# The reciprocal root in the collecting: a bit guess and Newton's steps on VectorE in place of ScalarE's Sqrt and a reciprocal

## The chip, the cores and the metric

The kernel runs on one core of one Trainium2 chip. Its engines work from queues of their own: TensorE (PE, with its weight loads as PEld), VectorE (DVE), ScalarE (ACT), GpSimd (POOL) and SyncE (SP, used here to issue DMAs). The metric is the device time of one execution in microseconds (us); the time of a kernel is the median of its runs.

## The reference

The input x has two sequences of 4096 tokens with 512 values each. What is computed, in float32 throughout:

```python
# attention: a linear layer W that learns while it reads, one step of descent per token
K, V, Q = x @ theta_K.T, x @ theta_V.T, x @ theta_Q.T
for each token t:                                  # per sequence, W and b start from W0, b0
    g = 2/512 * (W @ K[t] + b - V[t])
    W, b = W - 0.01 * outer(g, K[t]), b - 0.01 * g
    y[t] = W @ Q[t] + b
x = layernorm(x + y)                               # (x - mean) / sqrt(var + 1e-5), over 512 values
# feed-forward: one shared expert, and the best 2 of 8 routed experts for each token
shared = silu(x @ sW1 + sb1) @ sW2 + sb2
score  = sqrt(softplus(x @ routing_W.T + expert_bias))
routed = sum over the 2 experts e of the highest score:
             score[e] * (silu(x @ rW1[e] + rb1[e]) @ rW2[e] + rb2[e])
out = layernorm(x + shared + routed)
```

The change is in the last of these lines: the factor 1 / sqrt(var + 1e-5) of the second layernorm, for all tokens but those of the last chunk.

## The kernel before

**Chunks and steps.** The 4096 tokens of a sequence are cut into 32 chunks of 128, and both sequences go together, so a chunk c is two blocks of 128x512 (s = 0, 1). Within a chunk the recurrence is turned into matrix products with a small triangular inverse; from chunk to chunk the matrices W go on. `step(c)` (from L420) does this for chunk c, with the first layernorm at its end (`layernorm`, L278). Beside it run `prep(c+1)` (projections of the next chunk), `invert(c)` (VectorE's row operations on the inverse, L373), and `shared(c-1)` (shared expert and `router` of the chunk before). A helper, `interleave`, weaves these generators in proportion to amounts given by hand; each `yield` is a place where it may go over to another.

**Routed experts.** Chunks 0 to 22 form the first group and 23 to 30 the second (`GROUPS`). The router writes down which tokens go to which expert. When a group is complete, `plan` makes lists of tiles of 128 tokens with one expert each, and `routed` works through the tiles: POOL gathers tokens (L812) and weights (L818) by indirect DMA; TensorE turns the tokens (L827) and makes the first product (L836); ScalarE applies Silu (`he`, L840); TensorE makes the second product (`pye`, L847); VectorE evicts it with a bias (`o`, L850), and SP's queue stores it (L852). A weight buffer is fetched anew only after the L850 that read it. Chunk 31 is left out of the groups: `dense(31)` computes all eight experts for it and weighs them (Silu L705, products L702 and L713, sum L716), with its own layernorm.

**Collecting.** `collect(gr)` brings a group's results back, chunk by chunk. For chunk j+1 POOL fetches `acc`, which is x plus the shared expert (L882), and four gathered tiles `z` (L888; two sequences, two experts). For chunk j VectorE adds the four `z` to `acc`, each with its weight (L933). Then the mean and the variance are formed, in one of two ways. With `squares` set, the last sums also give the row totals, VectorE scales them to minus the mean (L939), and ScalarE takes the squares with their totals (L941). Otherwise VectorE uses its statistics instructions (L946, L947). The end of a chunk is the generator `finish` (from L895): variance plus epsilon (L898 or L900), ScalarE's Sqrt in place (L901), `yield`, VectorE's reciprocal (L903), with `squares` the product of mean and factor (L905), the scaling of `acc` (L908 on ScalarE, or L911 on VectorE), and the output's DMA on ScalarE's queue (L913).

**Where `finish` stands.** It is not run at once: `done` holds it, and the next chunk's loop calls it twice, ahead of its sums number 2 and 3 (`finish_at` is (2, 3)), or number 0 and 1 in the stage without `squares`. So the part up to the `yield` stands in VectorE's order ahead of one L933, and the rest ahead of the next. For the last chunk of a group both parts follow at once.

**Stages.** The first group is collected in three places: 14 chunks in steps 28 to 31 (4, 4, 4 and 2, with `squares`), and 9 beside the second group's routed tiles (without `squares`). The second group's 8 chunks are collected at the end beside `dense(31)` (with `squares`).

**Order.** For TensorE and VectorE the order of instructions is the order in which the program is written (`manual_schedule`), so an instruction that waits holds all behind it on its engine. The orders of ScalarE, POOL and SP are laid by a scheduler when the program is built. ScalarE's functions come in tables; the compiler puts an `ACT_TABLE_LOAD` ahead of a function whose table isn't the one loaded. Sqrt is used by both layernorms (L286), the router (L547) and `finish` (L901); Exp (L517) and Ln (L522) by the router; Silu at L638, L705 and L840.

Of the kernel before, what the change touches and what calls it, by code (L numbers as in the profile page):

```python
# [41 lines left out]
F32 = mybir.dt.float32  # L42
BF16 = mybir.dt.bfloat16
I32 = mybir.dt.int32
AF = mybir.ActivationFunctionType
ALU = mybir.AluOpType
# [60 lines left out]
def postln_block(ctx: ExitStack, tc: tile.TileContext, x, xT, thK, thV, thQ, w0, b0, masks, blk,  # L107
                 unit, order, rw, eb, w1s, b1s, w2s, b2s, b2e, wcat, out):
    nc = tc.nc
# [24 lines left out]
    sm = ctx.enter_context(tc.tile_pool(name="sm", bufs=2))  # L134
# [138 lines left out]
    for g, n in enumerate(GROUPS):  # L273
        groups.append(Group(g, sum(GROUPS[:g]), n))
        for i in range(n):
            of_step[groups[g].c0 + i] = groups[g]

    def layernorm(t, tag, c, s, scalar=False):  # L278

        st = sm.tile([P, 6], F32, tag=tag + "st", name=f"{tag}st_{c}_{s}")  # L280
        nc.vector.bn_stats(st, t[:, s, :])
        mv = sm.tile([P, 2], F32, tag=tag + "mv", name=f"{tag}mv_{c}_{s}", bufs=3)
        nc.vector.bn_aggr(mv, st)
        rstd = sm.tile([P, 1], F32, tag=tag + "rs", name=f"{tag}rs_{c}_{s}", bufs=3)
        nc.vector.tensor_scalar(rstd, mv[:, 1:2], EPS, None, ALU.add)
        nc.scalar.activation(rstd, rstd, AF.Sqrt)  # L286
        yield
        nc.vector.reciprocal(rstd, rstd)
        if scalar:
            shift = sm.tile([P, 1], F32, tag=tag + "sh", name=f"{tag}sh_{c}_{s}")  # L290
            nc.vector.tensor_scalar(shift, mv[:, 0:1], rstd, -1.0, ALU.mult, ALU.mult)
            nc.scalar.activation(t[:, s, :], t[:, s, :], AF.Identity, bias=shift, scale=rstd)
        else:
            nc.vector.tensor_scalar(t[:, s, :], t[:, s, :], mv[:, 0:1], rstd,
                                    ALU.subtract, ALU.mult)
        yield
# [578 lines left out]
    def collect(gr):  # L875

        got = {}

        def fetch(j):
            c = gr.c0 + j  # L880
            acc = cp.tile([P, B, D], F32, tag="acc", name=f"acc_{c}", bufs=4)
            nc.gpsimd.dma_start(out=acc,  # L882
                                in_=gr.base[j * T:(j + 1) * T].rearrange("(s p) d -> p s d", p=P))
            z = []
            for s in range(B):
                for k in range(K):
                    t = cp.tile([P, D], F32, tag=f"z{s}{k}", name=f"z_{c}_{s}_{k}")
                    nc.gpsimd.indirect_dma_start(  # L888
                        out=t, out_offset=None, in_=gr.ex,
                        in_offset=bass.IndirectOffsetOnAxis(ap=gr.sidx[:, j, s, k:k + 1], axis=0),  # L890
                        bounds_check=gr.tiles * P - 1, oob_is_err=False)
                    z.append(t)
            got[j] = acc, z

        def finish(c, acc, mean, var, on_scalar):  # L895

            if on_scalar:
                nc.vector.tensor_scalar(var, var, 1.0 / D, EPS, ALU.mult, ALU.add)  # L898
            else:
                nc.vector.tensor_scalar(var, var, EPS, None, ALU.add)  # L900
            nc.scalar.activation(var, var, AF.Sqrt)  # L901
            yield
            nc.vector.reciprocal(var, var)  # L903
            if on_scalar:
                nc.vector.tensor_tensor(mean, mean, var, ALU.mult)  # L905
            for s in range(B):
                if on_scalar:
                    nc.scalar.activation(acc[:, s, :], acc[:, s, :], AF.Identity,  # L908
                                         bias=mean[:, s:s + 1], scale=var[:, s:s + 1])
                else:  # L910
                    nc.vector.tensor_scalar(acc[:, s, :], acc[:, s, :], mean[:, s:s + 1],  # L911
                                            var[:, s:s + 1], ALU.subtract, ALU.mult)
            nc.scalar.dma_start(out=out[:, c * P:(c + 1) * P, :].rearrange("s p d -> p s d"),  # L913
                                in_=acc)
            yield

        fetch(0)
        yield 2.0
        done = iter(())
        for j in range(gr.n):  # L920
            c = gr.c0 + j
            if j + 1 < gr.n:
                fetch(j + 1)
            acc, z = got.pop(j)
            on_scalar = squares[0]
            mv = sm.tile([P, 2, B], F32, tag="fmv", name=f"fmv_{c}")
            mean, var = mv[:, 0], mv[:, 1]

            for i in range(B * K):
                s, k = i // K, i % K  # L930
                if i in finish_at[0]:
                    next(done, None)
                nc.vector.scalar_tensor_tensor(  # L933
                    acc[:, s, :], z[i], gr.cw[:, j, s, k:k + 1], acc[:, s, :], ALU.mult, ALU.add,
                    accum_out=mean[:, s:s + 1] if on_scalar and k == K - 1 else None)
                yield 0.9
            if on_scalar:

                nc.vector.tensor_scalar(mean, mean, -1.0 / D, None, ALU.mult)  # L939
                for s in range(B):  # L940
                    nc.scalar.activation(z[s * K], acc[:, s, :], AF.Square,  # L941
                                         bias=mean[:, s:s + 1], accum_out=var[:, s:s + 1])
            else:
                for s in range(B):
                    st = sm.tile([P, 6], F32, tag="fst", name=f"fst_{c}_{s}")
                    nc.vector.bn_stats(st, acc[:, s, :])  # L946
                    nc.vector.bn_aggr(mv[:, :, s], st)  # L947
            for _ in done:
                pass
            done = finish(c, acc, mean, var, on_scalar)  # L950
            yield 0.4
        for _ in done:
            pass
# [110 lines left out]
```

## Time and profile before

| | |
|---|---|
| median of 3 runs | 2687.22 us (2684.12 to 2687.95) |
| the profiled execution | 2680.63 us |
| its span, first to last instruction | 2678.8 us |
| mean granted clock of TensorE | 0.982 |
| busy: PE / PEld | 2549.3 / 1648.3 us |
| busy: DVE / ACT / POOL | 1375.0 / 743.4 / 984.5 us |
| instructions: DVE / ACT | 4024 / 1480 |
| finishes in the trace | 31, at 2155 to 2673 us |

Busy time in us, stage by stage, for the part of the span in which the collecting runs:

| stage | from : to (us) | PE | DVE | ACT | POOL |
|---|---|---|---|---|---|
| step 28 | 2143 : 2210 | 61.9 | 46.2 | 22.2 | 27.7 |
| step 29 | 2210 : 2277 | 62.8 | 44.1 | 23.2 | 28.9 |
| step 30 | 2277 : 2344 | 56.7 | 49.2 | 30.2 | 28.1 |
| step 31 | 2344 : 2400 | 38.2 | 23.6 | 15.7 | 26.7 |
| routed tiles | 2400 : 2609 | 181.4 | 79.3 | 82.3 | 118.7 |
| last stage | 2609 : 2679 | 50.8 | 40.4 | 47.0 | 35.2 |

The busy time of an engine is read against the length of the stage: TensorE fills 62 of 67 us in step 28, and in the last stage no engine is full on its own. What holds the work there is seen from the waits and from the chain, which is followed back from the last instruction, at each step to what released it. "Idle before, <-" in a row names what ended the idle time ahead of an instruction; "issue" is time for which the trace shows no wait. Times in the trace's rows count from the start of the span.

### The profile page before, as it was taken

What the parts mean: (1) busy time and instruction counts of PE and PEld (TensorE: products, weight loads), DVE (VectorE), ACT (ScalarE), POOL (GpSimd) and SP (SyncE); (2) the same over time, 40 slices, a digit from 0 to 9 for tenths busy, and PEclk for the clock granted to TensorE, in tenths of its full rate; (3) what the DMA queues carried; (4) which work ended last, traced back from release to release, by engine and by line L of the source; (5) the groups of instructions that cost most, each with busy time, mean ns of one, the idle gap of its engine ahead of it and who ended that gap; (6) DMA issues with size and microseconds to landing.
All of it is one profiled execution on the core that took longest, in us unless ns stands there. A gap on an engine that the chain in (4) does not pass through costs nothing.

```text
span 2678.8 us, 30957 instructions
## 1 busy us (share of the span) xinstructions
PE 2549.3 (95%) x10269; PEld 1648.3 (62%) x10269; DVE 1375.0 (51%) x4024; ACT 743.4 (28%) x1480; POOL 984.5 (37%) x819
## 2 busy tenths in 40 slices
PE   8999999999999999999998989999999999879887
PEld 6656666665666666566665767666676655445564
DVE  2566656656666566666565223232232466744336
ACT  1222222222222222222221313323233133434236
POOL 0232322233332223233234344343443444456554
PEclk9999999999999999999999999999999999989898
DMA  5122222222222222222223333442433446586676
GB/s 182 48 78 73 57 65 68 57 58 78 73 57 61 72 57 58 71 79 58 59 64 134 107 95 109 110 158 82 114 106 104 135 142 176 162 257 228 216 244 231
DMA packets 257711, 293.47 MB, mean 110 GB/s; under 512 B 158332, under 2 KB 171868, under 8 KB 253968
## 3 DMA queue, kind: packets, MB, share of 16 engines
q1 hardware_dynamic: 199536, 163.62, 20.6%
q0 software_dynamic: 49584, 111.61, 14.6%
q10 hardware_dynamic: 8432, 16.25, 1.8%
q8 instruction: 82, 1.34, 0.2%
q14 instruction: 77, 0.63, 0.1%
HBM read 345.43 MB, written 100.69 MB: 167 GB/s over the span
## 4 chain that ended last, share of the span: by engine, by line
PE 82%; DMA 5%; issue 4%; DVE 3%; ACT 3%; POOL 2%; SPq 0%; POOLq 0%; DVEq 0%; ACTq 0%
PE pkq L330 16%; PE pr L431 8%; PE pr L436 8%; PE pye L847 8%; PE po L447 7%; PE pw L491 7%; PE phe L836 7%; PE ph L619 4%; PE pa L343 4%; PE py L659 4%; PE pe L473 2%; PE po L485 2%; PE pg L827 2%; PE pz L412 1%; DMA wb<-wcat_in,widx 1%
## 5 line engine op out<-in xcount | busy, mean ns | idle before, releaser
L373 DVE SCALAR_TENSOR_TENSOR X<-L,X 128x31 f32<-128x31 f32 (+22 forms) x1472 | 418.2, 333 | 26.4 <-DMA L<-dL 9.5
L836 PEld LDWEIGHTS phe<-gT,wb 128*128 128x128 f32 x2208 | 275.2, 197 | 80.9 <-issue 76.1
L586 POOL DMA_INDIRECT gt<-code,ri x124 | 128.1, 1033 | 494.4 <-DVE ri L583 465.2
L850 DVE TENSOR_TENSOR o<-pye,wb 128x512 f32<-128x512 f32 x138 | 95.4, 692 | 412.8 <-PE pye L847 409.4
L836 PE MATMUL phe<-gT,wb 128*128 128x128 f32 x2208 | 279.0, 281 | 23.5 <-DMA wb<-wcat_in,widx 22.1
L847 PE MATMUL pye<-wb,he 128*128 128x512 f32 x552 | 271.8, 615 | 16.1 <-ACT he L840 15.0
L481 POOL PARTITION_ALL_REDUCE ar<-R x28 | 172.3, 6155 | 237.4 <-issue 180.9
L491 PE MATMUL pw<-R,K 128*128 128x512 f32 x496 | 239.4, 605 | 13.5 <-DVE x L486 12.6
L330 PE MATMUL pkq<-xT,thK 128*128 128x256 f32 x1024 | 242.9, 381 | 7.4 <-DMA thK<-thK_in 7.4
L447 PE MATMUL po<-W,kq 128*128 128x512 f32 x512 | 246.5, 604 | 0.0
L330 PE MATMUL pkq<-xT,thQ 128*128 128x256 f32 x1024 | 243.8, 382 | 1.0 <-DVE Z L414 1.0
L330 PEld LDWEIGHTS pkq<-xT,thK 128*128 128x128 f32 x1024 | 195.1, 191 | 80.4 <-issue 59.5
L818 POOL DMA_INDIRECT wb<-wcat_in,widx x138 | 147.0, 1065 | 262.1 <-DVE o L850 133.5
L431 PE MATMUL pr<-thV,xT 128*128 128x512 f32 x512 | 240.5, 593 | 0.0
L436 PE MATMUL pr<-W,kq 128*128 128x512 f32 x512 | 240.2, 592 | 0.0
L330 PEld LDWEIGHTS pkq<-xT,thQ 128*128 128x128 f32 x1024 | 189.7, 191 | 46.6 <-issue 24.9
L840 ACT ACTIVATE he<-phe,wb 128x128 f32<-128x128 f32 x276 | 87.1, 364 | 435.8 <-PE phe L836 434.1
L492 DVE TENSOR_TENSOR W<-pw,W 128x512 f32<-128x512 f32 x248 | 168.5, 689 | 73.0 <-PE pw L491 70.4
L337 ACT COPY kq<-pkq 128x256 f32<-128x256 f32 x256 | 82.9, 375 | 420.5 <-PE pkq L330 420.2
L812 POOL DMA_INDIRECT g<-gy,gidx x138 | 138.8, 1006 | 134.0 <-PE pg L827 105.9
L491 PEld LDWEIGHTS pw<-R,K 128*128 128x128 f32 x496 | 91.3, 191 | 137.1 <-issue 95.6
L847 PEld LDWEIGHTS pye<-wb,he 128*128 128x128 f32 x552 | 99.5, 192 | 120.4 <-issue 81.8
(209 smaller groups left out, 3429.8 us busy)
## 6 DMA issues: line engine op xcount, KB each, us to landing
ge<-o SPq DMA_DIRECT2D x138, 256.0 KB, 2.0
xT<-xT_in SPq DMA_DIRECT2D x32, 512.0 KB, 4.3
x<-x_in SPq DMA_DIRECT2D x32, 512.0 KB, 4.3
L<-dL SPq DMA_DIRECT2D x128, 128.0 KB, 2.8
gy<-x SPq DMA_DIRECT2D x31, 512.0 KB, 3.0
gb<-x SPq DMA_DIRECT2D x31, 512.0 KB, 3.4
acc<-gb POOLq DMA_DIRECT2D x31, 512.0 KB, 5.3
y_out<-acc ACTq DMA_DIRECT2D x31, 512.0 KB, 5.1
```

Source lines behind the costliest of these rows:

```text
L330: nc.tensor.matmul(ps[:, i].rearrange("p s t -> p (s t)"), th[:, dc, (ec + i) * P:(ec + i + 1) * P], xt[:, dc].rearrange("p s t -> p (s t) ...
L373: nc.vector.scalar_tensor_tensor(X[:, h, j + 1:], L[:, j + 1:, j], X[:, h, j:j + 1], X[:, h, j + 1:], ALU.mult, ALU.add)
L431: nc.tensor.matmul(ps, xt[:, dc, s, :], nthV_sb[:, dc, :], start=(dc == 0), stop=False)
L436: nc.tensor.matmul(ps, KQ[:, ec, s, 0, :], W[s][:, ec, :], start=False, stop=(ec == DC - 1))
L447: nc.tensor.matmul(ps, KQ[:, ec, s, 1, :], W[s][:, ec, :], start=(ec == 0), stop=False)
L481: nc.gpsimd.partition_all_reduce(ar, R, P, bass_isa.ReduceOp.add)
L491: nc.tensor.matmul(ps, K[s][:, ec, :], F[s], start=True, stop=True)
L492: nc.vector.tensor_tensor(W[s][:, ec, :], ps, W[s][:, ec, :], ALU.add)
L812: nc.gpsimd.indirect_dma_start(out=g_t[k], out_offset=None, in_=gr.y, in_offset=bass.IndirectOffsetOnAxis(ap=gr.gidx[:, k:k + 1], axis=0), ...
L818: nc.gpsimd.indirect_dma_start(out=wbuf[k % NW], out_offset=None, in_=wcat, in_offset=bass.IndirectOffsetOnAxis(ap=gr.widx[:, k:k + 1], ax ...
L836: nc.tensor.matmul(ps[:, hc, :], w[:, dc * HF + hc * P:dc * HF + (hc + 1) * P], t[:, dc, :], start=(dc == 0), stop=(dc == DC - 1))
L847: nc.tensor.matmul(ps, h[:, hc, :], w[:, O2 + hc * D:O2 + (hc + 1) * D], start=(hc == 0), stop=(hc == HC - 1))
```

## The change

In `finish` the Sqrt on ScalarE and VectorE's reciprocal after the `yield` go. In the Sqrt's place stands a new helper, `rsqrt`, that works on VectorE alone and leaves 1 / sqrt(var) in `var`: the bits of var as an integer are shifted right by one and taken from a constant, which gives a first guess g, and four rounds of g = g (1.5 - 0.5 v g g) follow, three instructions each. All 14 instructions are issued ahead of the `yield`. The layernorms of `step` and `dense` and the router's Sqrt stay as they are.

```diff
+    def rsqrt(v, name):
+
+
+        shape = list(v.shape)
+        g = sm.tile(shape, F32, tag="rsg", name=f"rsg_{name}")
+        nc.vector.tensor_scalar(g.bitcast(I32), v.bitcast(I32), 1, None, ALU.logical_shift_right)
+        nc.vector.tensor_scalar(g.bitcast(I32), g.bitcast(I32), -1.0, float(0x5f3759df),
+                                ALU.mult, ALU.add)
+        t = sm.tile(shape, F32, tag="rst", name=f"rst_{name}")
+        for i in range(4):
+            nc.vector.scalar_tensor_tensor(t, g, -0.5, v, ALU.mult, ALU.mult)
+            nc.vector.tensor_tensor(t, t, g, ALU.mult)
+            nc.vector.scalar_tensor_tensor(v if i == 3 else g, t, 1.5, g, ALU.add, ALU.mult)
...
                 nc.vector.tensor_scalar(var, var, EPS, None, ALU.add)
-            nc.scalar.activation(var, var, AF.Sqrt)
+            rsqrt(var, f"{c}")
             yield
-            nc.vector.reciprocal(var, var)
             if on_scalar:
                 nc.vector.tensor_tensor(mean, mean, var, ALU.mult)
```

## The prediction

> **What bounds the kernel now.** I read the chain of waits first, because the change moves work between engines and only the engine on the chain pays or gains.
>
> ```profile
> PE 82%; DMA 5%; issue 4%; DVE 3%; ACT 3%; POOL 2%; SPq 0%; POOLq 0%; DVEq 0%; ACTq 0%
> ```
>
> Over the whole span TensorE is the bound. But the reciprocal root of the collecting first runs at 2155 us (below), and from there on the chain changes hands: steps 28 to 31 (2143 to about 2400 us) are TensorE with waits for VectorE, the routed tiles of the second group (to 2609) are TensorE with waits for DMA and ScalarE, and the last stage (2609 to 2679, the dense chunk beside the second collecting) is a closed loop of VectorE and ScalarE. So each stage gets its own sum.
>
> Next, the views of two source lines, the Sqrt (L901) and the reciprocal after it (L903): instructions with their least, median and greatest ns, then for L903 what its engine sat idle for.
>
> ```profile
> L901 ACT ACTIVATE fmv<-fmv x31: 203/204/205, 2155.2 to 2672.8; 128x2 f32<-128x2 f32 x31
> L901 ACT ACT_TABLE_LOAD  x16: 1283/1283/1283, 2400.5 to 2655.7; - x16
> ...
> L903 DVE RECIPROCAL fmv<-fmv x31: 152/156/167, 2158.0 to 2673.0; 128x2 f32<-128x2 f32 x31
> its engine sat idle before it (us, times) until:
>   ACT fmv L901: 6.3, 8
> ```
>
> The reader is to see that VectorE waits for the Sqrt only 6.3 us in 31 uses, all in the last stage, although 16 of them load a table; and that none of the Sqrts in the steps (before 2400.5) loads one.
>
> Then one turn of the last stage, VectorE alone in order of time (start, duration, line; the bracket is idle time and its cause):
>
> ```profile
> 2641.13 0.17 DVE L898 TENSOR_SCALAR fmv<-fmv 128x2 f32<-128x2 f32 x1 [1.58 <-ACT z L941]
> 2641.24 0.75 DVE L933 SCALAR_TENSOR_TENSOR acc<-z,cw,acc 128x512 f32<-128x512 f32 x1
> 2643.00 0.17 DVE L903 RECIPROCAL fmv<-fmv 128x2 f32<-128x2 f32 x1 [1.01 <-ACT fmv L901]
> 2643.20 0.16 DVE L905 TENSOR_TENSOR fmv<-fmv 128x2 f32<-128x2 f32 x1
> 2643.28 0.74 DVE L933 SCALAR_TENSOR_TENSOR acc<-z,cw,acc 128x512 f32<-128x512 f32 x1
> ...
> 2648.49 0.17 DVE L898 TENSOR_SCALAR fmv<-fmv 128x2 f32<-128x2 f32 x1 [1.59 <-ACT z L941]
> ```
>
> A turn takes 7.36 us (2641.13 to 2648.49), of which 1.0 is the wait for the Sqrt. TensorE needs only 6.89 us per expert there (its first products start at 2620.15, 2627.04, 2633.92), so VectorE sets the pace.
>
> Last, who TensorE waited for in the routed tiles (2430 to 2609 us: total us, times, longest):
>
> ```profile
> PE pg L827 <- DMA g<-gy,gidx: 10.1, 3, 3.8
> PE pye L847 <- ACT he L840: 7.4, 8, 2.3
> PE phe L836 <- DMA wb<-wcat_in,widx: 5.4, 3, 2.5
> ```
>
> **The change, part by part.** Each of the 31 finishes loses one Sqrt on ScalarE (0.204 us), in 16 of them the table load before it and mostly the one that gives Silu its table back (1.283 each, about 40 us of ScalarE in all), and one reciprocal on VectorE. It gains 14 instructions on 128x2 on VectorE: two for the guess, three for each of four rounds.
>
> *Price of one.* The new shapes are not in the trace; the nearest rows are L903 and L905, 0.16 us each. Every new instruction needs the one before it, and a dependent pair starts 0.20 apart (2643.00 and 2643.20; 0.19 at 2166.68 and 2166.87), while an independent one follows after 0.08 (2643.20 and 2643.28). I take p = 0.195, so a block is 14 x 0.195 = **2.73 us**; the ends are 0.085 (if they overlapped like independent ones) and 0.22. The Trainium skill ("VectorE: DVE Perf Modes", Rules for kernel authors) speaks against the change: minimise the count of chained operations, not their semaphores. Its formula for a tensor_tensor, (N+151)/0.96 ns, gives 159 ns at N=2, so 2.23 us; the rows' spacing includes the dependence and I use it.
>
> *Price of the tables.* The skill ("ScalarE: Activation LUTs", What ACT_TABLE_LOAD costs) puts a switch of set at about 2.66 us, a load and a drain. This trace shows the load alone: at 2634.10 it starts, 1.28 later the Sqrt at 2635.39 runs. By the page a pair of switches is 5.3 us and a 2.73 us block would win; by the rows it is 2.57, on an engine that has room. In the last stage ScalarE's loads also start ahead of the wait, so VectorE sees 1.0. I go by the rows.
>
> *Last stage.* Now L905 starts 2.07 after L898. After the change the block follows L898 (0.20 later), its fourteenth instruction starts at 0.20+13p, L933 0.10 after it, L905 0.67 after that: 13p+0.97 = 3.50. **+1.43** per turn for the turns after finishes 1 to 5 (turn 7.36 to 8.8), **+1.78** after the sixth, where the Sqrt had come sooner (L903 at 1.52 after L898). The seventh (2662.57) had no wait: block less reciprocal, **+2.54**. The eighth is the serial end: L898 at 2672.57 to the scaling at 2673.41 was 0.84, and becomes 0.20+2.73+0.20, **+2.29**. Sum 7.15+1.78+2.54+2.29 = **+13.8**. The layernorm's Sqrt (L286, 2665.26) now loads its own table, in the 2.28 us that ScalarE idles before it: nothing; uncovered, +1.3. The loads of Silu go too, but that wait isn't VectorE's.
>
> *Routed tiles (gain).* When Sqrt and Silu swap tables there, TensorE's second product waits for `he`: 0.76 (2406), 0.55 (2431), four times 0.56, 2.29 (2546) and 1.90 (2474). The last stays: ScalarE's output DMA waits for L911, which comes later. The rest is 5.8. VectorE has room (67.3 us busy of 179), and mostly the block fits: eviction L850 0.6, L898's counterpart L900 and block 2.9, L933 0.7, against 4.22 between evictions. Twice (2468.55, 2544.42) L900 comes late and the next eviction, with POOL's weight fetch behind it, slips 1.8, some 0.4 on TensorE each. Net **-5**; ends -7.4 and 0.
>
> *Steps 28 to 31 (14 finishes).* VectorE's order is written by hand, so what stands behind a block waits for it: copies of N and Z, the router, W's updates, POOL's gathers after the sums. I followed each:
>
> - the first block of steps 29 and 30 (2213.15, 2280.07) is ahead of the router; 2.5 less some 1.2 idle before Z (L414), on which TensorE already waits 0.5: about +1.5 each.
> - the last two finishes of each step stand ahead of x (L486), on which TensorE waits: here step 29.
>
> ```profile
> 2239.36 0.17 DVE L898 TENSOR_SCALAR fmv<-fmv 128x2 f32<-128x2 f32 x1
> 2240.97 0.75 DVE L933 SCALAR_TENSOR_TENSOR acc<-z,cw,acc 128x512 f32<-128x512 f32 x1 [1.44 <-DMA z<-ge,sidx]
> 2241.63 0.68 DVE L486 TENSOR_TENSOR x<-po,x 128x512 f32<-128x512 f32 x1
> ```
>
>   The block of the finish before (2234.29) moves its scaling on ScalarE, hence the Squares queued behind it, hence this L898 to about 2241.0; a block, then L486 at 2244.6: +3.0. Step 30 (2307.84) the same, with 2.34 of DMA wait as cover: +2.1. Step 28 (2174.70) stands before W's updates: +2.7, and 0.5 that the block at 2155.05 hands POOL's gathers.
> - step 31: 2372.26 lies in a 3.1 idle, nothing; 2387.00 is ahead of the last layernorm, whose result TensorE takes with 0.2 to spare: +2.7.
>
> Sum 3.0+5.1+3.2+2.7 = **+14**, ends 0 (the covers hold) and +20. The order on ScalarE, POOL and SP isn't written by hand and may be laid anew: plus or minus 3.
>
> *Total.* 13.8 - 5 + 14 = **+23**; I take +22, as small delays overlap: the profiled execution of 2680.6 (span 2678.8) would be 2703. It lay 6.6 below the median of the runs, 2687.2, to which I add the same: **2709 us**.
>
> **Rivals.**
> 1. *The steps absorb their blocks.* For: TensorE waits for VectorE only some 32 us in 2130 to 2400. Against: exactly at L486, Z and the layernorm. 13.8 - 5 = +9: 2696.
> 2. *Pile-up.* The later sums free `z` buffers later, POOL's single queue gathers late, and DMA waits grow at L486 and the tiles. For: POOL waits 31.6 us for L933 in the steps. Against: it then also has idle. Gathers a block late in each of four steps, 11, and a tile stall more: about +37, 2724.
> 3. *Faster.* The price p decides: the last stage costs 106p - 6.9. If the 14 run overlapped at 0.085, it is +2.1, the steps nothing, and the tiles give all 7.4: -5.3, 2682. Break-even is p = 0.11 with a gain of 5. Against: every step of Newton's reads the last result, and dependent pairs show 0.19 to 0.20.
> 4. *The loads stay.* The router's Sqrts keep theirs; but between 2418 and 2665 no other Sqrt is left. Were they kept, no gain in the tiles: 2714, inside the range.
>
> **Chances.** Forecast with 4: 0.68; rival 1: 0.18; rival 2: 0.10; rival 3: 0.04. The range 2694 to 2726 takes in p, the ends of the steps and tiles, and rivals 1 and 2; it leaves out rival 3 and the tails. This kernel's measurement tells 0.2% (5.4 us) from none. Slower by over that: 0.90 (most of rival 1 with it); within: 0.07; faster: 0.03.
>
> **What would show it.** VectorE gains 31 x 13 = 403 instructions and some 60 to 70 us busy, in chains 0.195 apart; the loads at L901 are gone and Silu's (L840, 28) fall to about 19; TensorE's waits for `he` in the tiles fall from 7.4 to 2 or 3; the turn of the last stage is 8.8; L486 is later by 2 to 3 in each step. Chains at 0.1, or steps no longer than before, would prove me wrong.

## The result, and the profile after

The changed kernel takes **2733.84 us** (median of 4 runs, 2727.64 to 2737.63) against 2685.67 of the kernel before beside it (4 runs, 2684.02 to 2687.95): ratio 1.0166, 95% interval 1.0144 to 1.0188. It is slower, as forecast, but by about twice the forecast's +22, and outside its range. A second set of runs on another occasion gave +41.7 (1.0153, 1.0140 to 1.0167). The profiled execution took 2733.61 us (span 2731.8, mean granted clock 0.975 against 0.982).

Source lines up to 277 keep their numbers; those of the kernel's middle are 14 higher than before, those behind the removed reciprocal 13 higher. The new instructions are L283 to L290.

Page part 1 of the kernel after, and under it two lines of the views of L283 and L290 (least, median, greatest ns; first and last start):

```profile
PE 2563.3 (94%) x10269; PEld 1653.1 (61%) x10269; DVE 1437.2 (53%) x4427; ACT 704.6 (26%) x1423; POOL 982.4 (36%) x819
...
L283 DVE TENSOR_SCALAR rsg<-fmv x31: 168/169/297, 2159.7 to 2723.5; 128x2 int32<-128x2 int32 x31
...
L290 DVE SCALAR_TENSOR_TENSOR rsg<-rst,rsg x93: 160/161/229, 2160.6 to 2725.5; 128x2 f32<-128x2 f32 x93
```

VectorE has 403 more instructions and 62 us more of work; ScalarE has 39 us less, as the loads at the Sqrt are gone and Silu's at `he` fell from 28 to 20. TensorE has the same 10269 instructions in a span 53 us longer, and is busy with them 14 us longer. The chain of waits, which named TensorE over the whole span of the kernel before, reaches back only over the last scaling here and says nothing, so the stages have to be read from waits and turns.

One turn of the last stage, VectorE in order of time:

```profile
2675.09 0.17 DVE L912 TENSOR_SCALAR fmv<-fmv 128x2 f32<-128x2 f32 x1 [1.59 <-ACT z L954]
2675.29 0.29 DVE L283 TENSOR_SCALAR rsg<-fmv 128x2 int32<-128x2 int32 x1
...
2676.02 0.16 DVE L289 TENSOR_TENSOR rst<-rst,rsg 128x2 f32<-128x2 f32 x1
2676.22 0.16 DVE L290 SCALAR_TENSOR_TENSOR rsg<-rst,rsg 128x2 f32<-128x2 f32 x1
...
2678.10 0.75 DVE L946 SCALAR_TENSOR_TENSOR acc<-z,cw,acc 128x512 f32<-128x512 f32 x1
...
2683.96 0.17 DVE L912 TENSOR_SCALAR fmv<-fmv 128x2 f32<-128x2 f32 x1 [1.59 <-ACT z L954]
```

Chained instructions start 0.20 apart (2676.02, 2676.22), the block holds VectorE from 2675.29 to 2678.10, and the turn is 8.87 us, against 7.36 before. The wait for the Sqrt is gone and the one for ScalarE's squares (1.59) is what it was.

Whom TensorE waited for in steps 28 to 31 (us in total, times, longest); first the kernel before, 2133 to 2428 us, then the kernel after, the same stretch:

```profile
PE pq L566 <- DVE chosen L557: 9.6, 4, 3.0
...
PE pw L491 <- DVE x L486: 3.9, 3, 1.6
```

```profile
PE pq L580 <- DVE chosen L571: 15.3, 4, 5.2
PE pw L505 <- DVE x L500: 13.1, 3, 4.8
...
PE pw L505 <- DVE W L506: 3.4, 1, 3.4
```

Three waits grew: for the router's `chosen` (+5.7), for the attention's `x` (+9.2) and for W's update (0.8 before, in the timeline further down). And the same view of the kernel after for the routed tiles, 2463 to 2645 us:

```profile
PE phe L850 <- DMA wb<-wcat_in,widx: 11.7, 5, 5.0
PE pg L841 <- DMA g<-gy,gidx: 8.3, 3, 3.2
PE pye L861 <- ACT he L854: 5.2, 7, 2.0
```

The wait for `he` is smaller (7.4 before), and the one for weights has taken its place (5.4 before). Lining up TensorE's identical order of products in the two traces, the kernel after is 2.75 us late ahead of the first finish (2159 us, where the change has done nothing yet), 27 late at 2384, 33 at 2420, 36 when the last stage begins, and 48 at its last product (the whole span ends 53 later). One trace against one trace is not enough for a stage: two kernels below that do the same as the kernel before up to 2384 stand 5.6 late and 2.6 early there. So the stages were run apart.

### The profile page after: what moved, and what is told of

It reads as the page before. It is cut to its first block, busy times and chain, and to the rows that moved or that the text cites. A ratio compares the mean times of both kernels' runs of the same rounds, so it can differ in the third digit from the quotient of the medians.

```text
span 2731.8 us, 31339 instructions
## 1 busy us (share of the span) xinstructions
PE 2563.3 (94%) x10269; PEld 1653.1 (61%) x10269; DVE 1437.2 (53%) x4427; ACT 704.6 (26%) x1423; POOL 982.4 (36%) x819
## 5 line engine op out<-in xcount | busy, mean ns | idle before, releaser
L387 DVE SCALAR_TENSOR_TENSOR X<-L,X 128x31 f32<-128x31 f32 (+22 forms) x1472 | 409.1, 326 | 26.8 <-DMA L<-dL 9.9
L505 PE MATMUL pw<-R,K 128*128 128x512 f32 x496 | 244.9, 617 | 25.2 <-DVE x L500 21.7
L351 ACT COPY kq<-pkq 128x256 f32<-128x256 f32 x256 | 82.9, 375 | 432.1 <-PE pkq L344 432.0
L902 POOL DMA_INDIRECT z<-ge,sidx x124 | 131.1, 1057 | 118.2 <-DVE acc L946 59.7
```

The source lines that it names most:

```text
L387: nc.vector.scalar_tensor_tensor(X[:, h, j + 1:], L[:, j + 1:, j], X[:, h, j:j + 1], X[:, h, j + 1:], ALU.mult, ALU.add)
L505: nc.tensor.matmul(ps, K[s][:, ec, :], F[s], start=True, stop=True)
```

## The experiments

In the texts on record, theory L is the forecast's own terms (a block delays what stands behind it on VectorE), S what the traces suggest (much of the steps' loss is ScalarE's order laid anew), D that the stages aren't additive, and T that the tiles' gain is real.

**Each stage alone.** The staged kernels choose per finish, with one condition. It is shown for steps_only; in tiles_only it is `not on_scalar`, in last_only `c >= GROUPS[0]`.

```diff
-            rsqrt(var, f"{c}")
+            newton = on_scalar and c < GROUPS[0]
+            if newton:
+                rsqrt(var, f"{c}")
+            else:
+                nc.scalar.activation(var, var, AF.Sqrt)
             yield
+            if not newton:
+                nc.vector.reciprocal(var, var)
```

> The new root only in the 14 finishes of steps 28 to 31 (the first group's), Sqrt and reciprocal in the other 17. Base: the kernel before at 2685.7. Theory L (length: the forecast's own terms, a block only delays what stands behind it on VectorE): +14, 2700. Theory S (what the trace after reads: the steps cost about 24 less some 3 that the two profiled executions differ by ahead of the first finish; two of the stalls because the first Silu of the shared expert stands ahead of the router's Exp on ScalarE): +20 to +24, 2706 to 2710. Theory D (the stages aren't additive; the late end of step 31 makes the tiles late): +30 or more.

> The new root only in the 9 finishes of the routed tiles, Sqrt and reciprocal in the other 22. Theory L: -5, 2681 (table loads go, TensorE waits less for he). Theory S (the output DMA on ScalarE's queue waits for the later scaling and holds he, weight fetches come late): +8 to +12, 2694 to 2698. Theory D (the loss in the tiles was brought from the steps): -5 to 0.

> The new root only in the 8 finishes of the last stage, Sqrt and reciprocal in the other 23. All theories: +13.8 to +14.6, 2699.5 to 2700.3; turn of the stage 8.8 us. If much less, the last stage's loss depends on what goes before it.

| kernel | median, us | before, us | difference | ratio, 95% interval |
|---|---|---|---|---|
| steps_only | 2714.59 | 2686.99 | +27.6 | 1.0096, 1.0073 to 1.0119 |
| tiles_only | 2686.34 | 2686.99 | -0.6 | 0.9999, 0.9987 to 1.0011 |
| last_only | 2701.05 | 2686.99 | +14.1 | 1.0049, 1.0034 to 1.0064 |

The last stage costs what every theory said, the tiles neither the gain of L nor the loss of S, and the steps twice the forecast's +14. The sum, 41, is the repeated whole (41.7), so D is not needed, though the intervals (6 us either way for the steps, 3 for the tiles, 4 for the last stage) would hide a few us of it. The waits of TensorE in the tiles of tiles_only (2436 to 2616 us):

```profile
PE pg L841 <- DMA g<-gy,gidx: 8.3, 3, 3.1
PE phe L850 <- DMA wb<-wcat_in,widx: 6.6, 4, 3.0
PE phe L850 <- issue: 2.6, 1, 2.6
PE pye L861 <- DVE acc L952: 2.0, 1, 2.0
PE pye L861 <- issue: 1.8, 3, 0.6
PE pye L861 <- ACT he L854: 1.5, 4, 0.5
```

`he` fell from 7.4 to 1.5, as it should without the loads; but with the others the view adds up to 22.8, where the kernel before has 22.9 in its three rows. The likely reading is that TensorE reaches the next tile earlier and meets it unready.

**No root at all.** Sqrt, reciprocal and block are left out:

```diff
-            rsqrt(var, f"{c}")
             yield
```

> Neither Sqrt and reciprocal nor the block: the root is left out, the scaling uses the variance itself. A bound for what any cheaper root can bring. The order on ScalarE has Exp ahead of Silu. Theory S: the last stage is then set by TensorE's 6.89 per expert, 7 x 0.47 + 0.6 = -4; the tiles gain 0 (their wait for he is covered by the weights' DMA, as tiles_only showed); the steps 0: 2683. Theory T (the tiles' gain of 5 is real when no block stands against it): -9, 2678.

Measured 2692.43 against 2691.95: ratio 1.0000, 0.9988 to 1.0012. Even a root that costs nothing gains nothing. VectorE of this kernel in the last stage shows why:

```profile
2645.19 0.17 DVE L912 TENSOR_SCALAR fmv<-fmv 128x2 f32<-128x2 f32 x1 [1.59 <-ACT z L953]
2648.18 0.75 DVE L945 SCALAR_TENSOR_TENSOR acc<-z,cw,acc 128x512 f32<-128x512 f32 x1 [2.82 <-DMA z<-ge,sidx]
...
2654.05 0.17 DVE L912 TENSOR_SCALAR fmv<-fmv 128x2 f32<-128x2 f32 x1 [1.59 <-ACT z L953]
```

As soon as VectorE is faster it waits for the gathered `z`: six turns from 2624.04 to 2669.52 take 7.58 us on average; with the Sqrt six take 7.26 (2619.04 to 2662.57). VectorE's waits for gathered `z` from 2600 us on add up to 13.2 us, against 4.9 in the kernel before. In this order of calls the gathers are a second limit right beside the first. Both theories had a gain, and both were wrong.

**ScalarE's order.** In steps 29 and 30 of the changed kernel the scheduler had put half of the shared expert's Silu, with its table load, ahead of the router's Exp. This edit holds it behind, as it was before the change:

```diff
-        nc.scalar.activation(u, u, AF.Exp)
+        exp_of[c] = nc.scalar.activation(u, u, AF.Exp)
...
-        for hc in range(HC):
-            nc.scalar.activation(h[:, hc].rearrange("p s t -> p (s t)"), ps[:, hc, :],
-                                 AF.Silu, bias=b1_sb[:, hc:hc + 1])
+        with tc.issue_after(exp_of[c].ins):
+            for hc in range(HC):
+                nc.scalar.activation(h[:, hc].rearrange("p s t -> p (s t)"), ps[:, hc, :],
+                                     AF.Silu, bias=b1_sb[:, hc:hc + 1])
```

> The changed kernel, with the shared expert's two Silu held behind the router's Exp on ScalarE, as in the kernel before; nothing else is edited. Theory S: steps 29 and 30 each get back 2.3 to 3 us (the Exp no longer waits for a Silu and two table loads), 2833.8 is not touched otherwise: 2733.8 - 5 = 2729. Theory L (the order on ScalarE does not matter, only the block's length): 2733.8, within 1.

(The 2833.8 in it is a slip for 2733.8.) Measured 2723.54, ratio 1.0139 (1.0115 to 1.0164): 10 below the first runs of the changed kernel, but with overlapping intervals and from another set of runs. So both ran once more side by side, in five rounds:

> The changed kernel itself once more, beside the next run on the same chip, to size the order on ScalarE: +45 to +48 over the kernel before, ratio 1.017.

> The changed kernel with the shared expert's Silu held behind the router's Exp, beside after_again. Theory S (order costs about 10): 10 below after_again, with intervals that do not overlap. Theory L (its earlier gain was chance): within 3 of after_again.

Measured 2727.68 (1.0153, 1.0140 to 1.0167) and 2720.80 (1.0137, 1.0121 to 1.0153) against 2686.03: 6.9 apart, and again the intervals overlap. The last comparison took the steps alone, once as they are, once with the same edit, and once with two rounds of Newton's. In this third kernel Exp stands ahead of Silu too. Its text on record says that ScalarE's order is that of the second, which is not so throughout: copies of K and Q (L351) stand in other places among the scalings.

> The new root only in steps 28 to 31, once more, as the measure for the next two on the same chip: +24 to +28.

> As steps_again, with the shared expert's Silu held behind the router's Exp on ScalarE; the block of 14 and its places are the same. Theory S (order costs 5 to 10 there): +17 to +20. Theory L (the steps' excess over the forecast's +14 is all length, the order is worth nothing): within 2 of steps_again.

> The new root only in the steps, with two rounds (a block of 1.56 us, the root less exact); ScalarE's order is that of steps_pinned. Length alone, 1.17 us in some 6 places: 7 below steps_pinned, +10 to +13. If waits for DMA take half of it up: 3 below.

| kernel | median, us | over before (2689.41) | ratio, 95% interval |
|---|---|---|---|
| steps_again | 2712.81 | +23.4 | 1.0093, 1.0075 to 1.0112 |
| steps_pinned | 2709.03 | +19.6 | 1.0073, 1.0054 to 1.0092 |
| steps_r2 | 2705.02 | +15.6 | 1.0061, 1.0042 to 1.0080 |

By the medians the order is worth some 4 us in the steps, a little less than S put on it (5 to 10), and 7 or 10 in the whole kernel: the same sign three times, no comparison conclusive alone. (Two copies of K and Q change places in each of the two steps when Silu is held.) How it comes about is plain in the traces. ScalarE of steps_again in step 29, and TensorE's start on the router's `pq`:

```profile
2222.92 1.28 ACT L652 ACT_TABLE_LOAD   x1 [0.50 <-DVE lg L637]
2224.21 0.47 ACT L652 ACTIVATE h<-pht,b 128x256 f32<-128x256 f32 x1
2224.70 1.28 ACT L531 ACT_TABLE_LOAD   x1
2226.00 0.22 ACT L531 ACTIVATE u<-u 128x16 f32<-128x16 f32 x1
...
2232.01 0.19 PE L580 MATMUL pq<-chosen,before 128*128 128x8 bf16 x2 [5.08 <-DVE chosen L571]
```

The same place in steps_pinned:

```profile
2228.11 1.28 ACT L533 ACT_TABLE_LOAD   x1
2229.40 0.22 ACT L533 ACTIVATE u<-u 128x16 f32<-128x16 f32 x1
...
2235.45 0.20 PE L582 MATMUL pq<-chosen,before 128*128 128x8 bf16 x2 [2.85 <-DVE chosen L573]
```

One Silu and one more load, 1.78 us from 2222.92 to 2224.70, stand ahead of the Exp, and TensorE, which waits for what comes of it, waits 5.08 and not 2.85. That 2.2 in each of two steps is 4.4, near the 4 measured.

The length seems worth less than its microseconds: six instructions fewer save 4.0 in all (7 expected), while the eight that stay cost 15.6. The intervals of the two kernels overlap and their orders differ in those copies, so this is no measure of the slope. TensorE's waits for `x` in steps 28 to 31 go the same way: 4.6 us in no_root, 10.2 in steps_r2 and 13.8 in steps_pinned; the first eight instructions bring more of it than the next six.

**Two rounds everywhere.**

```diff
-        for i in range(4):
+        for i in range(2):
...
-            nc.vector.scalar_tensor_tensor(v if i == 3 else g, t, 1.5, g, ALU.add, ALU.mult)
+            nc.vector.scalar_tensor_tensor(v if i == 1 else g, t, 1.5, g, ALU.add, ALU.mult)
```

> The changed kernel with two of Newton's rounds, not four: a block of 8 instructions, 1.56 us and not 2.73 (the root is less exact). In its instruction order the router's Exp stands ahead of the shared expert's Silu on ScalarE again, as before the change. Theory S (of the 47 that the change costs, about 10 are that order; the rest is length, some 8 places in the last stage and 6 in the steps where a block's length is paid): 47 - 10 - 8 x 1.17 - 6 x 1.17 = +21, 2707. Theory L (order is worth nothing, the whole 47 is length and goes with it): 47 x 8/14 = +27 or, by places, 47 - 16 = +31, 2714 to 2718.

Measured 2711.36 against 2691.95: +19.4, ratio 1.0082 (1.0065 to 1.0099). This is near S's +21. L's lower value, +27, lies just outside the interval (+17.5 to +26.7), its upper one clearly.

**Step 28 alone.** The condition is `c < 3`, three finishes; the router's Exp keeps its place.

> The new root only in the three finishes that run in step 28; the router's Exp keeps its place. The forecast's term for step 28: +3.2. The traces after (step 28 longer by 6.0 to 7.7 at TensorE's first pb): +6 to +7. If later waits of DMA take it up again: 0 to 3.

Measured 2690.77 against 2686.03: ratio 1.0023, 1.0013 to 1.0033, or +3.5 to +8.9. That takes in the +6 to +7 of the traces; the forecast's +3.2 lies just below. TensorE's two waits ahead of W's products, and two of POOL's gathers of `z`, in the kernel before:

```profile
2174.84 1.12 PE L491 MATMUL pw<-R,K 128*128 128x512 f32 x2 [1.59 <-DVE x L486]
2176.76 1.98 PE L491 MATMUL pw<-R,K 128*128 128x512 f32 x4 [0.80 <-DVE W L492]
...
2159.26 1.00 POOL L888 DMA_INDIRECT z<-ge,sidx  x1 [3.47 <-DVE place L575]
...
2165.91 1.04 POOL L888 DMA_INDIRECT z<-ge,sidx  x1 [0.30 <-issue]
```

and in first_only, TensorE, POOL and VectorE:

```profile
2177.46 1.13 PE L505 MATMUL pw<-R,K 128*128 128x512 f32 x2 [4.15 <-DVE x L500]
2182.30 3.53 PE L505 MATMUL pw<-R,K 128*128 128x512 f32 x4 [3.72 <-DVE W L506]
...
2161.85 1.00 POOL L902 DMA_INDIRECT z<-ge,sidx  x1 [4.32 <-DVE place L589]
...
2168.55 1.04 POOL L902 DMA_INDIRECT z<-ge,sidx  x1 [0.30 <-issue]
...
2175.20 1.59 DVE L952 SCALAR_TENSOR_TENSOR acc<-z,cw,acc 128x512 f32<-128x512 f32 x2 [4.33 <-DMA z<-ge,sidx]
```

The step pays twice. The second wait grows by 2.9: the third block stands ahead of W's update, as forecast. The first grows by 2.6, through POOL: its queue waits at the gather of 2159.26 for VectorE, which the first block makes 2.6 late. (The trace names `place`, a router's instruction; a weighted sum, which frees a buffer of `z`, ends just ahead of it, and which of the two holds the gather is not shown.) Behind that gather the queue stores the router's list of rows and only then gathers the `z` that the sum ahead of `x` waits for: 4.33 us, and 1.89 in the kernel before. Together 5.5.

**TensorE's clock in the steps.** The rows above show one thing more: four of W's products take 3.53 us in first_only and 1.98 in the kernel before. The profile records which share of full speed TensorE is granted, full or half in these traces. Here are steps 28 and 29, cut at the same products in each trace: from and to, length, TensorE's busy time, granted clock (then DMA). First the kernel before, then first_only, then steps_again:

```profile
2159.16:2210.38 51.22, 48.08 (x156) 1.00 0.55 161
2210.38:2277.18 66.80, 62.56 (x222) 1.00 0.61 175
...
2159.21:2217.28 58.07, 49.45 (x157) 0.94 0.49 143
2217.28:2284.43 67.15, 62.55 (x222) 1.00 0.59 173
...
2158.43:2216.39 57.96, 50.89 (x157) 0.91 0.50 143
2216.39:2291.85 75.46, 65.82 (x222) 0.93 0.53 154
```

Where the blocks stand, TensorE waits longer, its clock falls, and the same products take longer; first_only has blocks in step 28 and none in step 29, and of the two its clock falls in step 28 alone. In steps_again TensorE runs at half clock from 2174.8 to 2185.1, from 2229.4 to 2236.3 and from 2256.8 to 2260.2 us, and each of these stretches begins within a long wait or some 1 us behind it. Over steps 28 to 31 (2159 to 2420 us of the kernel before, cut at the same products everywhere), in us:

| kernels | traces | TensorE waiting | TensorE busy |
|---|---|---|---|
| no block in the steps (before, no_root, tiles_only, last_only, before_fa12, before_fa13) | 6 | 38.9 to 46.1 | 218.0 to 223.2 |
| all blocks (after, after_again, after_fa12, steps_only, steps_again) | 5 | 56.6 to 59.6 | 231.6 to 235.4 |
| all blocks, order held (pinned, pinned_again, steps_pinned) | 3 | 51.8 to 52.5 | 229.5 to 230.7 |

Mean against mean, the steps' blocks cost 16 us of waiting and 12 of slower products; with ScalarE's order held it is 10 and 9. The three groups do not overlap, so the order shows here too, with some 6 us of waiting. That the waits bring the half clock is read from where it falls; no run changed the clock alone. No length of wait can be named for it: in step 29 a wait of 2.3 us is followed by half clock in tiles_only and not in the kernel before.

**The finish moved in the last stage.** VectorE idles 1.58 us there for ScalarE's squares with the next chunk's sums at hand. The call of `finish` is moved one sum on:

```diff
-    squares[0] = True
+    squares[0], finish_at[0] = True, (1, 2)
```

in the kernel before and in the changed one, and, in the kernel before, with (1, 3):

> The kernel before, with the last stage's finish called one weighted sum later: the sum stands in the 1.58 us that VectorE waits for ScalarE's Squares. Expected if VectorE and ScalarE's loop sets the pace there: turn 7.36 - 0.66 = 6.7, so TensorE's 6.89 sets it: 7 x 0.47 = -3.3, 2683.4. If TensorE or the gathers already set it: 0.

> The changed kernel with the same move: in the last stage the block begins one weighted sum later, while ScalarE squares. Expected if the turn is VectorE's instructions plus its wait for the Squares: 8.86 - 0.66 = 8.2, 7 x 0.66 = -4.6, 2729.2. If the longer block has put another wait in its place: 0.

> The kernel before, the last stage's finish begun after the first weighted sum and its scaling called after the third, so that sums stand in both waits (for the Squares and for the Sqrt). If VectorE's waits were all that is left there: as with (1, 2) or up to 2 lower, -6 to -8. If the gathers of z or TensorE's 6.89 set the stage: as with (1, 2), -4 to -6.

before_fa12 took 2685.34 and after_fa12 2727.35 against 2691.95: ratios 0.9984 (0.9972 to 0.9997) and 1.0141 (1.0122 to 1.0159). In after_fa12 TensorE's expert products, which follow VectorE's turns, start at 2661.55, 2669.66 and 2677.77, so the turn is 8.11 us and not 8.87, near the 8.2 expected. before_fa13 took 2681.15 against 2686.03, ratio 0.9984 (0.9976 to 0.9991), so the second move adds nothing that shows. Both kernels with the Sqrt and the moved call are **faster than both kernels of this study**, by 4 to 7 us against the one before. That gain is not from the root but from its place.

## Why the prediction was right or wrong

**Right: the price of an instruction, and the last stage.** The chain runs 0.195 to 0.20 apart. The formula of the Trainium skill ("VectorE: DVE Perf Modes", The TRN2 errata) gave 159 ns, which is what one instruction takes (160), and the spacing in the trace of the kernel before was the better guide to a chain. The turn was forecast at 8.8 and is 8.87; the stage alone costs +14.1, forecast +13.8. The loads of the Sqrt are gone, and rival 4 with them. That the block would lose against Sqrt and loads held: the pair of loads was 2.57 us by the rows, not the 5.3 that the Trainium skill ("ScalarE: Activation LUTs", Table sets: the hidden batching unit) gives for two switches.

**Wrong: the tiles' "Net -5".** They gain nothing (-3.5 to +3.0 by the interval). The step that failed is the one that credited TensorE with the whole of its shorter wait for `he` (5.8 of it): in tiles_only the wait fell as forecast, from 7.4 to 1.5, and came back elsewhere: 1.2 more for weights, 2.0 for VectorE's sums and 4.4 for which the trace names no cause, less 1.8 for tokens. In the changed kernel it fell to 5.2, and the wait for weights grew by 6.3. The forecast did see something of the kind in one place, the output DMA that waits for L911. In the trace after it stands ahead of `he` in ScalarE's order there:

```profile
2508.59 0.38 ACTq L926 DMA_DIRECT2D y_out<-acc  x1
2509.07 0.63 ACT L854 ACTIVATE he<-phe,wb 128x128 f32<-128x128 f32 x2 [5.15 <-DVE acc L924]
```

Whether the loss would be a gain with that DMA on another queue was not tried.

**Wrong: the steps' "Sum +14".** Alone they cost +23 to +28. The step that failed is that the sum counts waits alone: it put at nothing, without a reason, that TensorE's products themselves become slower. Over steps 28 to 31 they take 12 us longer, and 9 with the order held, at the half clock that comes with the longer waits. The waits were not undersized as a whole: with the order held they grow by 10, where the forecast had 14. A second term was mis-sized, the order on ScalarE, which "may be laid anew: plus or minus 3": it was, in the two steps where it hurts, for about 4 us by the medians of the steps alone (6 of waiting by the traces) and 7 to 10 in the whole. A third was too small in its place: "0.5 that the block at 2155.05 hands POOL's gathers" is 2.6. The terms "ahead of the router" (1.5 each) and W's 2.7 point the right way; W's wait grew by 2.9.

That covers do not hold when they are transfers which the same block delays is what rival 2 (pile-up) said of the gathers, at a chance of 0.10, and its 2724 is the rival nearest to the result. The nearness is in part luck: the tile stall in its sum does not show (the tiles alone cost nothing), and it has no term for the clock either.

**The sum.** By the measured parts: 14 + 0 + 23 to 28 = 37 to 42, against 42 to 48 measured of the whole. The rest is inside the intervals of the runs; whether a few us of it are real (late steps making the tiles' weights late) stays open.

**A floor the forecast missed.** Rival 3, faster, priced the last stage at 106p - 6.9, a gain of 6.9 for p at nothing. no_root, which is that case and has no block in the tiles either, gains 0: with `finish` called where it is, the gathers hold the last stage's turn at 7.6.

## What to carry to other kernels

Before pricing a replacement, ask what the removed operation costs: leave it out in one run. Here that gives 0, so with the calls where they are a chain in its place had nothing to gain. When a block is put into an order written by hand, follow it through the queues it feeds (here POOL's single queue, then a gather, then `x`): a DMA wait in front of the critical instruction is no cover if the block delays that DMA. A wait of TensorE can cost more than its length: look at the granted clock behind it, and compare the busy time of the same products in both traces. And where one engine's order is laid by a scheduler, a longer neighbour can change it: compare the orders, and hold the one that matters.

## What the runs showed that was not expected

- The length of VectorE's block alone changes ScalarE's order: with 14 instructions one Silu and its table load (1.28 us) stand ahead of the router's Exp in steps 29 and 30, with 8 or none they do not. The kernel's time shows it as 4 to 10 us.
- A delay of some 3 us in VectorE's order is paid twice within one step: 2.9 us at W's update and 2.6 through POOL's gathers, in the trace of first_only. The slower clock adds 1.4 us of busy time there.
- Over the four steps the same products of TensorE take 9 to 12 us longer with the blocks than without, though no block touches them. In step 28 the granted clock is 1.00 in all six traces without blocks and 0.91 in all eight with them.
- Without any root the last stage is no faster: VectorE's wait moves from the Sqrt (1.0 us a turn) to the gathered `z` (2.82 in the turn shown).
